# Turning x with 32x32 block transposes on VectorE, and a W stage in eight tiles of 32 rows

## The chip, the cores and the metric

One core of a Trainium2 chip runs the kernel in a single launch. The metric is the device time in microseconds (us), the median of three runs. The engines are TensorE (PE in the profile; its weight loads are listed apart as PEld), VectorE (DVE), ScalarE (ACT), GpSimd (POOL) and SyncE (SP), which here only issues DMA transfers. All data are f32.

## The reference

Two layers over x of 32 images x 128 channels x 64 x 64 pixels. The first layer is the part that matters here: a group norm, then a product with complex 64x64 "butterfly" matrices along both axes of each image, a mix of the channels at each of the 64 x 64 frequencies, the way back, and the sum with x.

```python
def tensor_product(x, tw1, tw2, increasing_stride):
    y = jnp.swapaxes(butterfly_lastdim(jnp.swapaxes(x, -1, -2), tw1, increasing_stride), -1, -2)
    return butterfly_lastdim(y, tw2, increasing_stride)

def _kop2d(x, weight, kd1, kd2, k11, k12, k21, k22):
    ...
    x_f = tensor_product(xc, _c(k11), _c(k12), False)
    w_f = tensor_product(wc, _c(kd1), _c(kd2), False) * math.sqrt(H * W)
    prod = jnp.einsum('bihw,oihw->bohw', x_f, w_f)
    out = tensor_product(prod, _c(k21), _c(k22), True)
    return jnp.real(out)

x = x + _L0_conv_ref(_gn(x), ...)
t = _to_tokens(x)
t = t + _L1_attn_ref(_ln_t(t), ...)
t = t + _L1_ffn_ref(_ln_t(t), ...)      # 8 experts, the best 2 of each token
```

A butterfly is a fixed 64x64 complex matrix, so `x_f` is a real image times one matrix along w and one along h. The change is in the computation of `x_f` alone. The second layer (attention over channels, a mixture of experts) comes after.

## The kernel before

The kernel has three parts, one after the other. The first computes the group norm and `x_f` of each image and stores it to DRAM (`xf`). The second loads `xf` by frequency, makes the frequency's channel matrix and mixes (L632, L654), and stores `pf`. The third goes back from `pf`, adds x and does the second layer (L877 and after). The change is in the first part, lines 131 to 563.

In the first part an image `xs[b]` is [128 channels, 4096 pixels]. Its steps, with the names that the profile shows:

- `load` (L312): eight DMA transfers by SP, into one of three buffers `x`.
- Statistics and norm: eight `bn_stats` on VectorE (L319), the mean over four channels by two small matmuls into a PSUM tile `gps` (L332 and L342), between them and after them short VectorE steps (L337 to L345), a power on POOL (L349), and the scaling in place: four VectorE instructions of 1024 pixels (L362; on ScalarE, L360, for the first four images).
- `turn_over` (L373): the image is turned, so that w lies on the partitions. Four pieces `pz`, each of eight TensorE transposes of 128 x 128, two image rows at a time. `turned` (L383): ScalarE copies each piece out of PSUM in four instructions, into `zs[b]` = [partition: w, once for each half of the channels; channel within its half; h].
- `along_w` (L396): the W stage. Eight pieces `pv`, each of 32 matmuls with 64 rows of contraction, 64 columns and 64 moving columns, placed in four tiles (two of rows by two of columns) of TensorE. The result of a piece is one PSUM tile of two banks. `w_out` (L407): ScalarE copies it into `vs[b]`.
- `along_h` (L418): the H stage. Eight pieces `pf`, each of eight matmuls of 128 x 128 x 128. `h_out` (L428): copied out of PSUM into `f`, six pieces by VectorE, two (`g % 4 == 3`) by ScalarE. `store` (L436): two DMA transfers a piece, by SP.

All PSUM tiles of the part come from one pool of four buffers (`ps`), two banks each, the whole of PSUM. The statistics' `gps` takes one from the first small matmul to the last VectorE step that reads it.

The order of the work is not written out by hand. Each step is added to a `Plan` with an engine, an assumed duration, a due time, the steps it comes after and the buffers that it takes and frees. `Plan.run` then lists the steps: an engine that is free takes the ready step with the earliest due time whose buffers are free. TensorE's steps stay in the order in which they were added (`on_pe`). The assumed durations and the due times (`SLOT` times a place in the loop) only set this order; on the chip an instruction waits for what it needs.

The loop over `s` makes a stage: image s is turned, image s - 1 goes through the W stage, image s - 2 through the H stage, in four quarters: one `pz`, two `pv`, two `pf`. The two small matmuls of image s + 1 stand in the third quarter, on either side of the `pz` and the `pv` (`norm_on_pe`).

The matrix `pw` holds the W stage's butterfly, [64 rows twice, real and imaginary, 64], made by `input_matrices` from a butterfly of a unit matrix (`unit`, `level`); in `unit`, for this butterfly, the even and the odd rows of h are first put in two halves, because a transpose takes two image rows.

Of the kernel before, what the change touches and what calls it, by code (L numbers as in the profile page):

```python
# [90 lines left out]
def kernel(  # L91
# [39 lines left out]
    pw = cp.tile([P, 2, n], F32, name="pw")  # L131
    ph = cp.tile([P, 2, n], F32, name="ph")
# [30 lines left out]
    with ExitStack() as ph1:  # L163
        pp = ph1.enter_context(tc.tile_pool(name="pp1", bufs=4, space=PSUM))
        xp = ph1.enter_context(tc.tile_pool(name="xp1", bufs=3))
        st = ph1.enter_context(tc.tile_pool(name="st1", bufs=1))
        bp = ph1.enter_context(tc.tile_pool(name="bp", bufs=1))
# [3 lines left out]
        SLOT = 27.5  # L171
# [26 lines left out]
        def unit(m, eng):  # L198
            def run():
                cur = tile_of["bf", m] = bp.tile([P, 2, n], F32, tag="bf", bufs=2, name=f"bf{m}_in")  # L200
                eng.tensor_tensor(cur[:, 0, :], ident[:, 0:n], ident[:, n : 2 * n], ALU.add)
                if m == 1:

                    eng.tensor_copy(
                        cur[lo, 0, :].rearrange("p (k r) -> p r k", r=2), ident[lo, 0:n].rearrange("p (r k) -> p r k", r=2)
                    )
                eng.memset(cur[:, 1, :], 0.0)
            return run
# [21 lines left out]
        def input_matrices():  # L230
            xa = tile_of["bf", 1]
            for half in (lo, hi):
                nc.vector.tensor_copy(pw[half], xa[hi])
# [133 lines left out]
        def turn_over(b, g):  # L367
            def run():
                ps = tile_of["pz", b, g] = pp.tile([P, 2, 512], F32, tag="ps", name=f"pz{b}_{g}")
                pv = ps.rearrange("w u (k c) -> w (u k) c", c=P)  # L370
                for k in range(8):
                    h = 2 * (8 * g + k)
                    nc.tensor.transpose(pv[:, k, :], xs[b][:, h * n : (h + 2) * n], ident)  # L373
            return run

        def turned(b, g, r):

            def run():
                if g == 0 and r == 0:
                    zs[b] = zp.tile([P, n, n], F32, tag="z", name=f"z{b}")  # L380
                pv = tile_of["pz", b, g].rearrange("w u (k c) -> w (u k) c", c=P)
                for half in range(2):
                    nc.scalar.copy(  # L383
                        zs[b][half * n : (half + 1) * n, :, 32 * r + 8 * g : 32 * r + 8 * g + 8],
                        pv[r * n : (r + 1) * n, :, half * n : (half + 1) * n].rearrange("w h c -> w c h"),
                    )
            return run

        def along_w(b, g):
            def run():  # L390
                ps = tile_of["pv", b, g] = pp.tile([P, 2, 512], F32, tag="ps", name=f"pv{b}_{g}")
                for k in range(8):
                    for half in range(2):
                        rows = slice(half * n, (half + 1) * n)
                        for r in range(2):
                            nc.tensor.matmul(  # L396
                                ps[r * n : (r + 1) * n, half, k * n : (k + 1) * n],
                                zs[b][rows, 8 * g + k, :], pw[rows, r, :], start=True, stop=True,
                            )
            return run  # L400

        def w_out(b, g):

            def run():
                if g == 0:
                    vs[b] = vp.tile([P, n, P], F32, tag="v", name=f"v{b}")
                nc.scalar.copy(  # L407
                    vs[b].rearrange("h w (a c) -> h w a c", a=2)[:, :, :, 8 * g : 8 * g + 8],
# [15 lines left out]
        def h_out(b, g):  # L424
            def run():
                f = tile_of["f", b, g] = fp.tile([P, 8, 2 * n], F32, tag="f", name=f"f{b}_{g}")
                copy = nc.scalar.copy if g % 4 == 3 else nc.vector.tensor_copy
# [29 lines left out]
        def piece_of_image(b, k):  # L457
# [3 lines left out]
                [("pz", b - 3, g) for g in range(4)] + [("x", b, k - 1), ("pf", b - 4, k)],  # L461
# [28 lines left out]
        def piece(kind, b, g, at):  # L490
            if not 0 <= b < B:
                return
            if kind == "pz":
                add(
                    ("pz", b, g), "PE", 1.0, at, turn_over(b, g), [("nm", b, k) for k in range(4)],
# [948 lines left out]
```

## Time and profile before

| | |
|---|---|
| median of 3 runs | 6062.12 us (6061.84 to 6064.63) |
| span of the profiled execution | 6062.4 us |
| granted TensorE clock, mean | 0.991 |
| TensorE busy over the whole span | 5891.6 us, 97% |
| first part, 60 to 912 us: TensorE / VectorE / ScalarE / POOL busy | 842.2 / 482.5 / 581.2 / 94.1 us of 852 |
| the same: memory traffic | 228 GB/s |
| second part, 912 to 2540 us: TensorE busy | 1623.8 us of 1628 |
| third part, 2540 to 6062 us: TensorE busy | 3399.0 us of 3522 |

The profile is one execution. "Busy" adds the times in which an engine has an instruction in work; matmuls are pipelined, so a busy TensorE is not one at its peak, and the time of one record (220 ns for the W stage) is longer than the distance to the next. In a timeline the columns are start, length, engine, line, operation, output<-inputs, count; square brackets hold the idle time ahead of it and what ended it. "Issue" is idle time in which the engine waited for nothing that the profile shows.

In the first part, sums and means of the groups from 60 to 912 us:

| line, engine | what | count | mean ns of one |
|---|---|---|---|
| L373 PE | transposes `pz` | 952 | 274 |
| L383 ACT | copies of `pz` into `z` | 480 | 580 |
| L396 PE | W stage `pv` | 15,795 | 220 |
| L407 ACT | copies of `pv` into `v` | 248 | 1015 |
| L418 PE | H stage `pf` | 3936 | 278 |
| L428 DVE / ACT | copies of `pf` into `f` | 185 / 61 | 1216 / 1013 |
| L319 DVE | statistics | 224 | 684 |
| L362 DVE | scaling of x | 112 | 840 |

### The profile page before, as it was taken

How to read it: one execution, taken by the hardware profiler on the slowest of the kernel's cores; microseconds unless marked ns; L12 is line 12 of the kernel's file. 1: busy time of each engine (PE TensorE's matmuls, PEld its weight loads, DVE VectorE, ACT ScalarE, POOL GpSimd, SP SyncE). 2: the span in 40 equal slices, each digit the busy share in tenths (PEclk: the TensorE clock that was granted, in tenths of full speed). 3: DMA queues.
4: the chain of work that ended last, by engine and by line, in shares of the span. 5: the costliest groups of instructions: out<-in, count | busy, mean ns of one | idle time of the engine just before them, and what ended most of it. 6: DMA issues, size and time to landing. Idle time of an engine off the chain costs nothing.

```text
span 6062.4 us, 219265 instructions
## 1 busy us (share of the span) xinstructions
PE 5891.6 (97%) x95372; PEld 4677.6 (77%) x95372; DVE 4221.2 (70%) x7696; ACT 3756.5 (62%) x7057; POOL 4191.0 (69%) x3765
## 2 busy tenths in 40 slices
PE   7999999999999999889999999999999999999998
PEld 7999999999999999776666666666666666666654
DVE  5565545555555555448878787787878878787878
ACT  7666664555555555366667667666766766676663
POOL 2110006666666666428898898989989898998988
PEclk9999999999999999999999999999999999999999
DMA  6767666666666666632313222231322223132100
GB/s 200 238 224 237 234 214 193 172 173 172 172 174 171 171 171 172 160 107 77 92 56 102 67 88 81 72 97 57 101 68 84 84 64 104 57 97 71 65 27 28
DMA packets 555044, 756.74 MB, mean 125 GB/s; under 512 B 58592, under 2 KB 319712, under 8 KB 549984
## 3 DMA queue, kind: packets, MB, share of 16 engines
q1 hardware_dynamic: 551856, 738.76, 41.0%
q8 instruction: 749, 12.27, 0.9%
q0 software_dynamic: 896, 2.62, 0.1%
q14 instruction: 215, 1.76, 0.1%
q10 hardware_dynamic: 1328, 1.32, 0.1%
HBM read 406.93 MB, written 335.54 MB: 122 GB/s over the span
## 4 chain that ended last, share of the span: by engine, by line
PE 88%; ACT 7%; issue 2%; DVE 1%; POOL 1%; DMA 1%; SPq 0%; ACTq 0%; POOLq 0%; DVEq 0%
PE pe L1296 28%; PE m L654 17%; PE g L632 9%; PE pf L418 7%; PE pu L877 6%; PE pp L1145 4%; PE py L899 4%; PE pg L1072 4%; PE pv L396 3%; PE px L1283 2%; ACT xn L1273 2%; ACT u L887 2%; PE pz L373 1%; PE pt L1021 1%; ACT z L383 1%
## 5 line engine op out<-in xcount | busy, mean ns | idle before, releaser
L1296 PE MATMUL pe<-ew_sb,xT 128*128 128x512 f32 x4096 | 1948.4, 597 | 18.6 <-DVE tm L1307 15.1
L1307 DVE TENSOR_TENSOR tm<-pe,oh 128x512 f32<-128x512 f32 x2028 | 1346.6, 684 | 478.9 <-PE pe L1296 456.6
L1332 POOL TENSOR_TENSOR tm<-tm 128x512 f32<-128x512 f32 x1014 | 1285.0, 1284 | 202.6 <-DVE tm L1307 199.3
L1296 PEld LDWEIGHTS pe<-ew_sb,xT 128*128 128x128 f32 x4096 | 701.6, 191 | 523.4 <-issue 400.1
L643 DVE COPY f<-g 128x1024 f32<-128x1024 f32 x508 | 622.3, 1225 | 644.4 <-PE g L632 644.2
L654 PE MATMUL m<-f,s 128*64 128x64 f32 x32768 | 1068.9, 224 | 1.1 <-ACT f L643 0.8
L654 PEld LDWEIGHTS m<-f,s 128*64 128x64 f32 x32768 | 999.0, 138 | 62.4 <-issue 1.5
L600 POOL COPY s<-l 128x512 f32<-128x512 f32 x512 | 547.2, 1105 | 526.4 <-issue 509.7
L643 ACT COPY f<-g 128x1024 f32<-128x1024 f32 x508 | 514.7, 1013 | 556.4 <-PE g L632 530.1
L1335 POOL TENSOR_TENSOR tk<-tk,tm 128x256 f32<-128x256 f32 x1014 | 753.9, 743 | 79.5
L1333 POOL TENSOR_TENSOR tm<-tm 128x512 f32<-128x512 f32 x507 | 650.3, 1283 | 39.8
L887 ACT COPY u<-pu 64x512 f32<-64x512 f32 x960 | 556.3, 579 | 135.1 <-PE pu L877 121.6
L632 PE MATMUL g<-c,wst 9*128 9x128 f32 x16256 | 599.6, 283 | 1.7 <-issue 1.5
L632 PEld LDWEIGHTS g<-c,wst 9*128 9x128 f32 x16256 | 503.0, 186 | 36.2 <-issue 1.5
L349 POOL TENSOR_TENSOR grstd<-gms,mhalf 128x1 f32<-128x1 f32 x32 | 17.8, 555 | 737.8 <-DVE gms L345 737.8
L1158 ACT ACTIVATE pp<-pp,m 128x128 f32<-128x128 f32 x1024 | 440.9, 431 | 124.2 <-PE pp L1145 99.2
L602 POOL TENSOR_SCALAR s<-l 128x512 f32<-128x512 f32 x256 | 511.3, 1997 | 0.0
L877 PEld LDWEIGHTS pu<-qw,r 128*128 128x128 f32 x3840 | 455.1, 193 | 62.8 <-ACT u L887 49.0
L877 PE MATMUL pu<-qw,r 128*128 128x128 f32 x3840 | 475.8, 277 | 25.1 <-ACT u L887 25.1
L1289 ACT COPY xT<-px 128x512 f32<-128x512 f32 x256 | 150.2, 587 | 563.2 <-PE px L1283 560.1
L418 PE MATMUL pf<-ph,v 128*128 128x128 f32 x4096 | 491.2, 278 | 6.2 <-issue 1.4
L418 PEld LDWEIGHTS pf<-ph,v 128*128 128x128 f32 x4096 | 467.0, 192 | 16.0 <-ACT z L383 7.1
(169 smaller groups left out, 8569.6 us busy)
## 6 DMA issues: line engine op xcount, KB each, us to landing
xf<-f SPq DMA_DIRECT2D x512, 256.0 KB, 3.3
pf<-o SPq DMA_DIRECT2D x1024, 128.0 KB, 3.3
l<-xf SPq DMA_DIRECT2D x1012, 128.0 KB, 3.2
r<-pf SPq DMA_DIRECT2D x504, 256.0 KB, 4.7
x<-in_x_dram SPq DMA_DIRECT2D x256, 256.0 KB, 4.5
y<-in_x_dram SPq DMA_DIRECT2D x32, 2048.0 KB, 9.3
out_dram<-so SPq DMA_DIRECT2D x256, 256.0 KB, 2.2
tw<-in_tw_dram SPq DMA_DIRECT2D x6, 384.0 KB, 7.5
```

Source lines behind the costliest of these rows:

```text
L418: nc.tensor.matmul(pl[:, j * P : (j + 1) * P], vs[b][:, 8 * g + j, :], ph.rearrange("h r m -> h (r m)"), start=True, stop=True,)
L600: nc.gpsimd.tensor_copy(dst, src)
L632: nc.tensor.matmul(pg[g // 2][:, g % 2, m * P : (m + 1) * P], wst[rows, 16 * half + 4 * t + m, :], c[rows].rearrange("r h k -> r (h k)"), ...
L643: copy(f.rearrange("i m (g o) -> i m g o", g=2), tile_of["g", w, half, t][k].rearrange("i g (o m) -> i m g o", o=4))
L654: nc.tensor.matmul(ps[hh * n : (hh + 1) * n, q, :], s[:, h].rearrange("i k b -> i (k b)")[:, B * r : B * r + n], f[:, h, r, :], start=(r = ...
L877: nc.tensor.matmul(ps[:, k, :], rs[b, e][:, k * P : (k + 1) * P], qw.rearrange("w r m -> w (r m)"), start=True, stop=True,)
L887: nc.scalar.copy(u[r * n : (r + 1) * n, :, oh * n + 8 * e : oh * n + 8 * e + 8], ps[oh * n : (oh + 1) * n, :, r * n : (r + 1) * n].rearran ...
L1296: nc.tensor.matmul(ps, tile_of["xT", b, i // 4][:, i % 4, :], ew_sb[:, es, :].rearrange("d e c -> d (e c)"), start=True, stop=True,)
L1307: nc.vector.tensor_tensor(tile_of["tm", b, i // 2][:, i % 2, es, :], tile_of.pop(("pe", b, i, half)).rearrange("p (e c) -> p e c", c=P), t ...
L1332: nc.gpsimd.tensor_tensor(tm[:, k, 0:4, :], tm[:, k, 0:4, :], tm[:, k, 4:8, :], ALU.add)
L1333: nc.gpsimd.tensor_tensor(tm[:, :, 0:2, :], tm[:, :, 0:2, :], tm[:, :, 2:4, :], ALU.add)
L1335: nc.gpsimd.tensor_tensor(t[:, lo : lo + 2, :], t[:, lo : lo + 2, :], tm[:, :, m, :], ALU.add)
```

## The change

The image is no longer turned by TensorE and ScalarE. Four VectorE instructions an image (`nc.vector.transpose`, pieces `zo`) turn 32 x 32 blocks from SBUF to SBUF: the 32 values of half an image row in 32 channels change places. A block transpose leaves each group of 32 channels on its own 32 partitions, so `zs[b]` becomes [partition: 32 * channel group + w within half a row, channel within its group, half, h].

The W stage's contraction over 64 values of w is therefore two halves of 32, summed in PSUM (`start` for the first, `stop` for the second), with 32 rows of contraction at a time: eight tiles of TensorE, four groups of rows by two of columns, and twice as many matmuls. The four groups of rows write to four PSUM banks, two tiles of the `ps` pool. A piece is four times as many matmuls as before (128) and makes two PSUM tiles, so an image has four pieces.

`pw` grows to hold, on each group of 32 partitions, both halves of the matrix (eight small copies in place of two), and the reordering in `unit` goes. `pw` and `ph` move from the pool of constants to one that ends with the first part.

ScalarE copies four of the eight `pf` pieces instead of two, VectorE four instead of six. In a stage the order on TensorE is now: two W pieces, four H pieces, two W pieces, four H pieces; the two small statistics matmuls stand on either side of the second pair of W pieces. The assumed durations and `SLOT` (27.5 to 23.0) are changed with it. The loads of x wait for the last `zo` of the image three before, where they waited for its `pz`.

```diff
-    pw = cp.tile([P, 2, n], F32, name="pw")
-    ph = cp.tile([P, 2, n], F32, name="ph")
...
+        pw = st.tile([P, 2, 2, n], F32, name="pw")
+        ph = st.tile([P, 2, n], F32, name="ph")
...
-        SLOT = 27.5
+        SLOT = 23.0
...
-                if m == 1:
-
-                    eng.tensor_copy(
-                        cur[lo, 0, :].rearrange("p (k r) -> p r k", r=2), ident[lo, 0:n].rearrange("p (r k) -> p r k", r=2)
-                    )
...
-            for half in (lo, hi):
-                nc.vector.tensor_copy(pw[half], xa[hi])
+            for q in range(4):
+                for half in range(2):
+                    nc.vector.tensor_copy(pw[32 * q : 32 * q + 32, half], xa[n + 32 * half : n + 32 * half + 32])
...
-        def turn_over(b, g):
-            def run():
-                ps = tile_of["pz", b, g] = pp.tile([P, 2, 512], F32, tag="ps", name=f"pz{b}_{g}")
-                pv = ps.rearrange("w u (k c) -> w (u k) c", c=P)
-                for k in range(8):
-                    h = 2 * (8 * g + k)
-                    nc.tensor.transpose(pv[:, k, :], xs[b][:, h * n : (h + 2) * n], ident)
-            return run
-
-        def turned(b, g, r):
...
-                    nc.scalar.copy(
-                        zs[b][half * n : (half + 1) * n, :, 32 * r + 8 * g : 32 * r + 8 * g + 8],
-                        pv[r * n : (r + 1) * n, :, half * n : (half + 1) * n].rearrange("w h c -> w c h"),
-                    )
+        def turned(b, k):
+
+            def run():
+                if k == 0:
+                    zs[b] = zp.tile([P, 32, 2, n], F32, tag="z", name=f"z{b}")
+                nc.vector.transpose(
+                    out=zs[b][:, :, :, 16 * k : 16 * k + 16].rearrange("w c u h -> w h u c"),
+                    in_=xs[b][:, k * 1024 : (k + 1) * 1024].rearrange("c (h u w) -> c h u w", u=2, w=32),
+                )
             return run
 
         def along_w(b, g):
-            def run():
-                ps = tile_of["pv", b, g] = pp.tile([P, 2, 512], F32, tag="ps", name=f"pv{b}_{g}")
+
+            def run():
+                ps = [pp.tile([P, 2, 512], F32, tag="ps", name=f"pv{b}_{g}_{k}") for k in range(2)]
+                tile_of["pv", b, 2 * g], tile_of["pv", b, 2 * g + 1] = ps
                 for k in range(8):
                     for half in range(2):
-                        rows = slice(half * n, (half + 1) * n)
-                        for r in range(2):
-                            nc.tensor.matmul(
-                                ps[r * n : (r + 1) * n, half, k * n : (k + 1) * n],
-                                zs[b][rows, 8 * g + k, :], pw[rows, r, :], start=True, stop=True,
-                            )
+                        for q in range(4):
+                            rows = slice(32 * q, 32 * q + 32)
+                            for r in range(2):
+                                nc.tensor.matmul(
+                                    ps[q // 2][r * n : (r + 1) * n, q % 2, k * n : (k + 1) * n],
+                                    zs[b][rows, 8 * g + k, half, :], pw[rows, half, r, :],
+                                    start=(half == 0), stop=(half == 1),
+                                )
             return run
...
-                copy = nc.scalar.copy if g % 4 == 3 else nc.vector.tensor_copy
+                copy = nc.scalar.copy if g % 2 else nc.vector.tensor_copy
...
-                [("pz", b - 3, g) for g in range(4)] + [("x", b, k - 1), ("pf", b - 4, k)],
+                [("zo", b - 3, 3), ("x", b, k - 1), ("pf", b - 4, k)],
...
+            if kind == "zo":
+                add(
+                    ("zo", b, g), "DVE", 1.2, at, turned(b, g),
+                    [("nm", b, g), ("zo", b, g - 1)] + [("pv", b - 2, k) for k in range(4)], (), ("x",) if g == 3 else (),
+                )
+            elif kind == "pv":
+                add(("pv", b, g), "PE", 2.0, at, along_w(b, g), [("zo", b, k) for k in range(4)] + ["wi"], ("ps", "ps"))
...
-                piece("pz", s, g, at)
-                for k in range(2):
-                    piece("pv", s - 1, 2 * g + k, at + 0.04 + 0.04 * k)
+                piece("zo", s, g, at)
+                if g % 2 == 0:
+                    for k in range(2):
+                        piece("pv", s - 1, g + k, at + 0.04 + 0.08 * k)
```

`w_out` copies each of the two PSUM tiles of a piece as before, one ScalarE instruction a tile, eight an image.

## The prediction

> **What bounds the kernel now.** I read the chain of waits first (88% TensorE), then the stretches: the first part ends near 932 us. The stretch of one image in mid-part, from one start of `pf` piece 0 to the next, shows who is full.
>
> ```profile
> core 0: us, PE busy (x) PEld busy (x) DVE busy (x) ACT busy (x) POOL busy (x), PEclk, DMA share, GB/s
> 551.97:579.39 27.42, 27.32 (x676) 26.29 (x676) 15.94 (x24) 18.90 (x27) 0.55 (x1) 1.00 0.73 242
> ```
>
> TensorE works 27.32 of 27.42 us; VectorE (15.9) and ScalarE (18.9) have room. So in this part an image costs what TensorE's stream costs, and 32 images make up the part after a lead-in. The timeline of that image shows the stream; four such quarters make an image:
>
> ```profile
> 555.53 0.91 PEld L373 LDWEIGHTS pz<-ident,x 128*128 128x128 f32 x8
> 556.61 1.96 PEld L396 LDWEIGHTS pv<-pw,z 64*64 64x64 f32 x128 [0.17 <-issue]
> 558.63 3.65 PEld L418 LDWEIGHTS pf<-ph,v 128*128 128x128 f32 x32
> 562.20 0.91 PEld L373 LDWEIGHTS pz<-ident,x 128*128 128x128 f32 x8
> ```
>
> From start to start: `pz` 1.08, two `pv` pieces 2.02, two `pf` pieces 3.57, together 6.67 us. Four quarters are 26.68; the rest of 27.42, 0.74, are the two statistics matmuls (`gps`). One more reading: an f32 matmul is two weight loads and two matmul records (64 `pv` matmuls: x128 and x128), a transpose one of each.
>
> The third view is where TensorE waits for nothing that has a name. Weight loads at two places of the timeline:
>
> ```profile
> 207.63 1.64 PEld L418 LDWEIGHTS pf<-ph,v 128*128 128x128 f32 x14
> 210.53 1.64 PEld L418 LDWEIGHTS pf<-ph,v 128*128 128x128 f32 x14 [1.26 <-issue]
> ...
> 817.44 1.95 PEld L396 LDWEIGHTS pv<-pw,z 64*64 64x64 f32 x124 [0.17 <-issue]
> 820.30 0.19 PEld L396 LDWEIGHTS pv<-pw,z 64*64 64x64 f32 x4 [0.91 <-issue]
> ```
>
> The stream stops in the middle of a piece, with no semaphore. I counted the weight-load and matmul records before each unnamed stop over 0.3 us between 60 and 912 us. There are eight (0.34 to 1.34 us), and all eight counts leave remainder 193 when divided by 256; none of the thirty-odd stops that a semaphore explains does. The instruction queue's row fits (packets, MB, share of the DMA engines):
>
> ```profile
> q8 instruction: 749, 12.27, 0.9%
> ```
>
> 749 packets of 16,384 bytes over 2 x 95,372 records: 64 bytes a record, 256 records a packet. So TensorE reads its program in blocks of 256 records. The packets' times say how early: a block starts to arrive just after the boundary one block before its own is passed, takes 0.98 us (median; 0.88 to 3.1), and at the eight stops work resumed 1.22 to 1.57 us after the arrival. One block is ahead, then, and no more. From passing a boundary to being able to pass the next took 3.47 to 4.71 us at the eight stops, mean 4.1. Call this time L. Before, it costs next to nothing (18.9 us of unnamed waits of `pv` loads in all, most of them 0.17 us changes of tile), because an image has 1352 records, 5.3 blocks in 27.4 us.
>
> **The change, part by part.** All against the profiled execution: span 6062.4 us, 0.3 us over the runs' median.
>
> *Transposes leave TensorE:* 4 x 1.08 = 4.32 us an image less.
>
> *W stage.* Before, four records start 6.6 ns apart and the next four follow 58.4 ns after: four 64x64 tiles run side by side, a round of 64 columns lasts 58.4. 512 records / 4 x 58.4 = 7.48 us an image. After, 512 matmuls are 1024 records in eight tiles: 8 x 6.6 = 53 ns of starts fit into a round, 1024 / 8 x 58.4 = 7.48 again. The row for four row groups at once is L632 (9 rows, 128 columns): a round each 111.6 ns, as long as one record of L418; row groups do run together.
>
> [...]
>
> *Longer blocks.* A half image is now 512 W records in one run, then four `pf` pieces. A change of tile form costs 0.35 us a round trip (0.095 + 0.048 entering, 0.108 + 0.101 leaving), four times an image before, twice now. Without program reading a half is 3.74 + 0.35 + 7.14 = 11.23, an image 22.46 + 0.74 = 23.2 us.
>
> *Reading the program.* W records, loads counted, go from 1024 to 2048 an image, the transposes' 64 disappear: 2312 in all, nine blocks. A half's W run is 1024 records, so it passes four boundaries. At full rate a block lasts 0.93 us, far under L. The first boundary finds its block present; each of the next three waits L from the one before: 0.93 + 3 L instead of 3.74. No row shows L in a run that always starves. Lower bound: the shortest pieces, start 0.75 (after allowing 48 records that the sequencer is ahead), arrival 0.88, use 1.2: 2.9 us. Upper: the longest stop's 4.7. The eight stops are the long ones by selection, and the traffic gets thinner (some 6.3 MB an image over 41 us, 153 GB/s, against 242), so I take 3.6. Half: 0.93 + 10.8 + 0.35 + 7.14 = 19.2; image 38.4 + 0.74 = 39.2.
>
> [...]
>
> *Clock.* A mostly idle TensorE is slowed:
>
> ```profile
> 2592.28:2595.69 3.41, 0.81 (x28) 0.81 (x29) 0.00 (x0) 0.00 (x0) 0.00 (x0) 1.00 1.02 246
> 2595.69:2599.11 3.42, 3.42 (x72) 3.42 (x70) 1.38 (x2) 0.00 (x0) 0.00 (x0) 0.50 0.75 181
> ```
>
> After 24% work the next 3.41 us have half the clock. A starved W run works 0.93 of 3.6 us, 26%, so some `pf` runs will start slow: from 0 to 3.4 us lost a half (two such windows); I take 1.15, a third, 2.3 an image. Image: 41.5, that is 14.1 more.
>
> *VectorE* gets four 128x1024 block transposes an image and gives two of six L428 copies to ScalarE. No row shows a block transpose.
>
> ```profile
> L600 POOL COPY s<-l 128x512 f32<-128x512 f32 x512 | 547.2, 1105 | 526.4 <-issue 509.7
> L428 DVE COPY f<-pf 128x1024 f32<-128x1024 f32 x192 | 231.1, 1217 | 173.9 <-PE pf L418 164.8 <-ACT v L407 3.9 <-DMA xf<-f 2.3
> L362 DVE TENSOR_SCALAR x<-x,gms,grstd 128x1024 f32<-128x1024 f32 x112 | 87.0, 840 | 19.3 <-POOL grstd L349 19.3
> ```
>
> Bounds: 0.84 (L362, same tile) and 2.2 (twice L600); 1.22 as L428, a plain pass of that size. The rest: 8 x 0.684 statistics, 0.37, 0.7 small, 4 x 0.745 (L362, four in 2.98), 4 x 1.22 = 14.4; with transposes 19.3, at worst 23.2, hidden under 41.5. ScalarE falls to 8 x 1.015 + 4 x 1.013 = 12.2. Neither sets the end.
>
> *New wait.* `gps` holds one of four PSUM slots through both W pieces of the second half (28 images), and these take two each: the second tile of the last piece waits for ScalarE's first L407 copy: 0.22 (the last record's length), 0.13 (until a copy starts, L428 after `pf`), 1.01, 0.05 (until TensorE goes on, L632 after L643) = 1.4 us. Behind it on TensorE stand that piece, `gps` and four `pf`; ScalarE's next copies and VectorE wait for those. While the program starves it is covered (L leaves 2.7 us idle a block); without that cover it costs 1.4.
>
> *Queues and lead-in.* SP issues the same 8 loads and 16 stores an image; the loads' wait moves from `pz` to the transposes, which end in the same stage. q8 gets 120 blocks more, 2 MB. Eight small copies into `pw` instead of two: 6 x 0.23, once. The first image's W stage stood alone (39.4 to 61.8 us) and becomes about 25: lead-in +5 together.
>
> Sum: 31 x 14.1 + 5 = 442; 6062.4 + 442 = 6504 us. Own range: L 2.9 and no slow clock, image 35.0, gives 6302; L 4.7 and 3.4 a half, image 52.6, gives 6847.
>
> **The rivals.**
> First, faster: reading keeps ahead (the eight stops are chance, or a block can be asked for earlier in a run). Then an image is 23.2 + 1.4 = 24.6 in 28 images, 23.2 in three: -28 x 2.8 - 3 x 4.2 + 5 = -86, 5976 us. It decides when L is under 0.93 us. For: 27.4 us of nearly full TensorE lose 4.3. Against: the remainders. A slow transpose (2.2 us, load 23.2 plus waits, say 26.7 an image) would leave 6045.
> Second, slower otherwise: eight tiles run only four at a time, reading hidden: +7.5 an image, 32.1 with the wait; 31 x 4.7 + 5 = 151, 6213. Against: L632.
>
> **How the numbers follow.** Starved reading 0.80, the first rival with its slow form 0.13, the second 0.07. Prediction 6504. The first rival lies outside; below 6200 nothing else does, and I cut the top at 6720, about where L 4.4 with 2 us of slow clock a half stands (image 48.0, 6703). A difference under 0.2% (12 us) can't be told from none: faster 0.12, within 0.01, slower 0.87.
>
> **What would show it.** The W runs should stop with "issue" as the only cause, three times a half, 2.7 us each, 256 records apart; q8 near 870 packets; TensorE's busy share of the part near 60%; PEclk under 1.0 in slices that were 9; VectorE waiting for `pf`. If W runs last 3.8 us with rounds of 58 ns, I am wrong and the time is near 5976; if rounds last 117 ns with no stops, the second rival.

## The result, and the profile after

| | before | after |
|---|---|---|
| median | 6062.44 us | 6707.59 us (6704.58 to 6712.38) |
| ratio, 95% interval | | 1.1066 (1.105 to 1.1081) |
| span of the profiled execution | 6062.4 us | 6702.5 us |
| first `pf` matmul | 61.8 us | 90.1 us |
| mean image: first to last `pf` record, divided by 31 | 28.04 us | 47.68 us |
| first matmul of the second part to the end | 5129.9 us | 5132.7 us |

The changed kernel is 645 us slower; the forecast was 442. In the two traces the difference of 640.1 us is 31 x 19.64 = 609 for the images, 28.3 ahead of the first `pf`, and 2.8 behind the part. So it is all in the first part, and the other two parts were left as they were. (The first to the last `pf` record holds the end of the last stage too; from the first `pf` of the first image to that of the last, the mean image is 0.45 to 0.46 us less in every run below, so the differences are the same.)

The stretch of one image in mid-part, from one first W piece to the next, in the profile of the changed kernel (columns as in the fence of before):

```profile
core 0: us, PE busy (x) PEld busy (x) DVE busy (x) ACT busy (x) POOL busy (x), PEclk, DMA share, GB/s
506.63:552.28 45.65, 33.06 (x1158) 31.53 (x1157) 21.66 (x26) 11.75 (x12) 5.07 (x14) 0.78 0.42 142
```

Where TensorE filled 27.32 of 27.42 us it now fills 33.06 of 45.65, with the clock at 0.78 in place of 1.00. VectorE (21.7) and ScalarE (11.8) have half the time free, memory moves 142 GB/s in place of 242. No engine and no queue is full, yet an image takes 46 us. The weight loads of that image in the timeline of the changed kernel say what it waits for:

```profile
506.63 1.88 PEld L384 LDWEIGHTS pv<-pw,z 32*64 32x64 f32 x170
511.22 1.66 PEld L384 LDWEIGHTS pv<-pw,z 32*64 32x64 f32 x128 [2.70 <-issue]
515.78 2.08 PEld L384 LDWEIGHTS pv<-pw,z 32*64 32x64 f32 x128 [2.91 <-issue]
519.25 1.51 PEld L384 LDWEIGHTS pv<-pw,z 32*64 32x64 f32 x86 [1.39 <-issue]
520.88 8.03 PEld L408 LDWEIGHTS pf<-ph,v 128*128 128x128 f32 x64
528.83 0.30 PEld L328 LDWEIGHTS gps<-gmv,gmean 128*128 128x128 f32 x2
529.15 2.54 PEld L384 LDWEIGHTS pv<-pw,z 32*64 32x64 f32 x232
534.98 0.35 PEld L384 LDWEIGHTS pv<-pw,z 32*64 32x64 f32 x32 [3.29 <-issue]
536.52 1.59 PEld L384 LDWEIGHTS pv<-pw,z 32*64 32x64 f32 x96 [1.19 <-ACT v L397]
538.45 2.08 PEld L384 LDWEIGHTS pv<-pw,z 32*64 32x64 f32 x128 [0.34 <-issue]
542.47 0.52 PEld L384 LDWEIGHTS pv<-pw,z 32*64 32x64 f32 x24 [1.94 <-issue]
```

Read the counts first: 128 weight loads stand between most of the stops, which with their 128 matmuls are 256 records, one block of the program. A W run stops three times, for 1.4 to 3.3 us, with "issue" as the cause. The one stop with another name (`v` L397, 1.19 us) is the new PSUM wait. From 60 to 1560 us I counted all unnamed stops over 1 us: 174, and all 174 at a record count (weight loads, matmuls and TensorE's semaphore instructions) that leaves 193 when divided by 256. From passing such a boundary to passing the next took 4.23 us in the mean: 1.74 until the block starts to arrive, 1.11 to arrive, 1.38 until work resumes. The 10% and 90% points are 3.47 and 5.20.

The waits of the changed kernel from 200 to 1400 us, sorted by their sum (engine, line, what it waited for, total, times, longest):

```profile
ACT v L397 <- PE pv L384: 585.1, 103, 9.6
PEld pv L384 <- issue: 327.3, 143, 4.7
DVE f L418 <- PE pf L408: 325.9, 66, 13.7
...
PEld pv L384 <- ACT v L397: 22.8, 21, 1.2
```

ScalarE waits for W pieces and VectorE for H pieces; TensorE waits 327 us for its own program and 23 us for ScalarE. The slices and the instruction queue on the page of the changed kernel:

```profile
PE   5777767779999999999799999999999999999998
...
PEclk8777777778999999999899999999999999999999
...
q8 instruction: 868, 14.22, 0.9%
```

The first nine slices (168 us each) are 5 to 7, where all but the first were 9, with a clock of 7 to 8; 868 packets stand for 2 x 110,732 records and 804 semaphore instructions, 256 a packet again, and are 119 more than before.

### The profile page after: what moved, and what is told of

Same layout as the page of the kernel before. It is cut to its first block, busy times and chain, and to the rows that moved or that the text cites. A ratio compares the mean times of both kernels' runs of the same rounds, so it can differ in the third digit from the quotient of the medians.

```text
span 6702.5 us, 249448 instructions
## 1 busy us (share of the span) xinstructions
PE 6111.2 (91%) x110732; PEld 4885.6 (73%) x110732; DVE 4381.7 (65%) x7765; ACT 3525.8 (53%) x6609; POOL 4188.4 (62%) x3765
## 4 chain that ended last, share of the span: by engine, by line
PE 84%; issue 8%; ACT 5%; DVE 2%; POOL 1%; DMA 1%; SPq 0%; ACTq 0%; POOLq 0%; DVEq 0%
PE pe L1279 25%; PE m L637 15%; PE g L615 8%; PE pf L408 8%; PE pv L384 7%; PE pu L860 5%; PE pp L1128 4%; PE py L882 4%; PE pg L1055 3%; PE px L1266 1%; ACT xn L1256 1%; ACT u L870 1%; PE pt L1004 1%; PE po L1325 1%; ACT tk L1009 1%
## 5 line engine op out<-in xcount | busy, mean ns | idle before, releaser
L1279 PE MATMUL pe<-ew_sb,xT 128*128 128x512 f32 x4096 | 1946.0, 597 | 19.6 <-DVE tm L1290 16.1
L384 PE MATMUL pv<-pw,z 32*64 32x64 f32 x32768 | 518.1, 281 | 408.1 <-issue 383.4
L384 PEld LDWEIGHTS pv<-pw,z 32*64 32x64 f32 x32768 | 470.1, 171 | 449.1 <-issue 413.9
L397 ACT COPY v<-pv 128x1024 f32<-128x1024 f32 x256 | 248.0, 1015 | 727.7 <-PE pv L384 727.7
L408 PE MATMUL pf<-ph,v 128*128 128x128 f32 x4096 | 579.1, 313 | 2.3 <-ACT v L397 2.2
L408 PEld LDWEIGHTS pf<-ph,v 128*128 128x128 f32 x4096 | 568.9, 228 | 6.2 <-issue 1.4
```

The source lines that it names most:

```text
L384: nc.tensor.matmul(ps[q // 2][r * n : (r + 1) * n, q % 2, k * n : (k + 1) * n], zs[b][rows, 8 * g + k, half, :], pw[rows, half, r, :], sta ...
L408: nc.tensor.matmul(pl[:, j * P : (j + 1) * P], vs[b][:, 8 * g + j, :], ph.rearrange("h r m -> h (r m)"), start=True, stop=True,)
L1279: nc.tensor.matmul(ps, tile_of["xT", b, i // 4][:, i % 4, :], ew_sb[:, es, :].rearrange("d e c -> d (e c)"), start=True, stop=True,)
```

## The experiments

Theory A, the prediction's: TensorE reads its program in blocks of 256 records, one ahead; where 256 records are worked off in less than about 4.2 us it stands still, and the standing still halves its clock. Rival B: matmuls in eight tiles of 32 rows are slow in themselves. Rival C: the long blocks and the PSUM slots they take. Rival D: the block transposes on VectorE. The runs, with the image as above, the program's blocks in an image, and the share of mid-part in which the clock was halved:

| run | median us | ratio to before (95%) | image us | blocks | half clock |
|---|---|---|---|---|---|
| before | 6062.4 | | 28.04 | 5.3 | 0% |
| after | 6707.6 | 1.105 to 1.108 | 47.68 | 9.0 | 53% |
| e1 W in quarters | 6618.4 | 1.090 to 1.094 | 45.27 | 9.0 | 34% |
| e2 half the matmuls | 6181.7 | 1.019 to 1.022 | 31.01 | 5.0 | 27% |
| e3 128 moving columns | 6619.7 | 1.091 to 1.094 | 45.18 | 9.0 | 23% |
| e4 before, matmuls split | 6763.1 | 1.114 to 1.118 | 49.88 | 9.3 | 29% |
| e9 before, 128 columns | 6223.7 | 1.025 to 1.028 | 33.07 | 5.3 | 0% |
| e5 `gps` elsewhere | 6689.2 | 1.102 to 1.106 | 47.12 | 9.0 | 51% |
| e6 W in eighths | 6397.2 | 1.054 to 1.058 | 38.23 | 9.0 | 7% |
| e8 transposes twice | 6722.4 | 1.108 to 1.111 | 48.04 | 9.0 | 54% |
| e7 half the W records | 6069.9 | 1.0005 to 1.0024 | 28.05 | 5.0 | 5% |
| f1 and GpSimd scales | 6053.7 | 0.998 to 1.000 | 27.44 | 5.0 | 5% |
| f2 the same in eighths | 6178.9 | 1.018 to 1.021 | 31.28 | 5.0 | 1% |
| f3 f1, weights later | 6037.7 | 0.995 to 0.997 | 27.12 | 5.0 | 2% |

**e1: the long blocks undone.**

```diff
-                if g % 2 == 0:
-                    for k in range(2):
-                        piece("pv", s - 1, g + k, at + 0.04 + 0.08 * k)
+                piece("pv", s - 1, g, at + 0.04)
```

> The changed kernel (6707.6 us, an image 47.7 us) with the longer blocks undone: one W piece (512 records), then two pf pieces, four times an image; all instructions the same. Theory A (program reading: a block of 256 records can be passed 4.2 us after the one before, mean of 174 stops of the changed kernel, and the idling halves the clock): still nine blocks an image, but two boundaries a run in place of four, so one or two stops a quarter; image 39.5 us at full clock, 44.5 with slow windows, so 6445 to 6605 us. Rival B (matmuls in eight tiles of 32 rows are themselves slow): the same work in another order, 6690 to 6720. Rival C (the long blocks, by the PSUM slots they take, are the whole loss): near or under 6062.

6618.4 us, 13 above A's range; image 45.27. The long blocks cost 2.4 us an image, an eighth of the loss, so C isn't the whole of it, and B's "no change" is out by 70 us. A W run of 512 records now stops once (mean 2.5 us); of the 134 unnamed stops over 1 us from 60 to 1560 us, 133 are at remainder 193.

**e2: half the matmuls.** The second half of the contraction is left out.

```diff
-                    for half in range(2):
+                    for half in range(1):
...
-                                    start=(half == 0), stop=(half == 1),
+                                    start=True, stop=True,
```

> The changed kernel with only the first half of the W stage's contraction: 256 matmuls an image in place of 512, same eight tiles, same blocks, PSUM slots and copies. It leaves out the sum over the other 32 values of w. Theory A: 1288 records an image, five blocks; a W run of 512 records passes two boundaries and stops once; image 28.7 to 30.6 us, so 6100 to 6160 us, and every unnamed stop over 1 us at remainder 193. Rival B: the W run is half as long as now (14.9 to 7.4 us a half image) because its matmuls are half, image 32.8, near 6230, with no stops at block ends. Rival C: blocks and slots are unchanged, so at most the work left out is won (3.7 us an image): 6590.

6181.7 us, 22 above A's range and 48 below B's time; image 31.01. What tells them apart is in the trace of this run, two W runs:

```profile
612.32 1.07 PEld L384 LDWEIGHTS pv<-pw,z 32*64 32x64 f32 x90 [1.54 <-issue]
...
622.64 2.54 PEld L384 LDWEIGHTS pv<-pw,z 32*64 32x64 f32 x228
627.84 0.54 PEld L384 LDWEIGHTS pv<-pw,z 32*64 32x64 f32 x28 [2.66 <-issue]
```

A W run of half an image now has one unnamed stop over 1 us (0.92 in the mean, 2.4 us each) in place of 2.7, and 58 of these 59 are at remainder 193. The eight tiles, the slots and the copies are those of the changed kernel, and 16.7 us an image are gone, where the work left out is 3.7 by the prediction's rate and 5.4 by the measured one (512 matmul records at 10.6 ns, see below).

**e3: more work in the same records.** If the reading sets the W run, work can be added for nothing.

```diff
-        pw = st.tile([P, 2, 2, n], F32, name="pw")
+        pw = st.tile([P, 2, 3, n], F32, name="pw")
...
+                                m = 2 if k < 7 else 1
                                 nc.tensor.matmul(
-                                    ps[q // 2][r * n : (r + 1) * n, q % 2, k * n : (k + 1) * n],
-                                    zs[b][rows, 8 * g + k, half, :], pw[rows, half, r, :],
+                                    ps[q // 2][r * n : (r + 1) * n, q % 2, k * n : (k + m) * n],
+                                    zs[b][rows, 8 * g + k, half, :],
+                                    pw[rows, half, r : r + m, :].rearrange("w m c -> w (m c)"),
```

> The changed kernel with seven of eight W matmuls given 128 moving columns in place of 64 (the second 64 are written over by the next matmul): as many records, nearly twice the TensorE work in the W stage (14.0 us an image at full rate in place of 7.5). Theory A: the work fits into the time that the reading takes (1.87 us of 4.2 a block) and the clock stays higher: W run 0.93 x 2 + 3 x 4.2 = 14.5 us, pf at full clock 7.1, image 44.8 (43 to 47.7): 6610 us (6550 to 6710), so not slower than the changed kernel, and a granted clock over 0.74 in the first part. Rival B (TensorE's work in the tiles sets the run): 6.5 to 15 us an image more, 6915 to 7190.

6619.7 us: 88 us *faster* than the changed kernel, with nearly twice the columns in its W stage. The third part of `pw` repeats its real half, so that each widened matmul has 128 columns to read. B, as a cost of the tiles' work, is out: more work in the tiles can't make a run shorter that the tiles' work sets. Mid-part of the changed kernel and of this run, the same stretch (us, PE, PEld, DVE, ACT, POOL busy, PEclk, DMA share, GB/s):

```profile
300.00:1100.00 800.00, 573.56 (x19238) 548.02 (x19237) 357.06 (x428) 195.07 (x202) 50.96 (x137) 0.74 0.41 136
```

```profile
300.00:1100.00 800.00, 631.27 (x20412) 595.56 (x20412) 378.76 (x454) 207.83 (x215) 50.33 (x135) 0.88 0.43 146
```

TensorE is busier, the clock goes from 0.74 to 0.88, and more records pass in the same time. From 100 to 1350 us a W run, `gps` included, is 15.1 us long in the mean (15.0 in the changed kernel), and a run of `pf` takes 7.5 in place of 8.9. So the gain is the clock of the H stage.

**e4 and e9: the records alone, in the kernel before.** e4 splits each W matmul of before in two of 32 moving columns:

```diff
-                        for r in range(2):
-                            nc.tensor.matmul(
-                                ps[r * n : (r + 1) * n, half, k * n : (k + 1) * n],
-                                zs[b][rows, 8 * g + k, :], pw[rows, r, :], start=True, stop=True,
-                            )
+                        for j in range(2):
+                            for r in range(2):
+                                nc.tensor.matmul(
+                                    ps[r * n : (r + 1) * n, half, k * n + 32 * j : k * n + 32 * j + 32],
+                                    zs[b][rows, 8 * g + k, :], pw[rows, r, 32 * j : 32 * j + 32], start=True, stop=True,
+                                )
```

> The kernel before with each W matmul split into two of 32 moving columns: 2376 records an image in place of 1352 (9.3 blocks), the same columns, the same four 64-row tiles, transposes, order and PSUM slots. Theory A: image 41 to 46 us in place of 27.4: 6500 to 6660 us, with unnamed stops at remainder 193. Rivals B and C, which need the eight tiles or the long blocks: 6050 to 6130.

6763.1 us, over the top of A's range by 103: slower than the changed kernel, without a block transpose, a 32-row tile or a longer W block. In its timeline a quarter with twice the records:

```profile
716.17 0.91 PEld L373 LDWEIGHTS pz<-ident,x 128*128 128x128 f32 x8
717.24 3.37 PEld L397 LDWEIGHTS pv<-pw,z 64*64 64x64 f32 x222 [0.17 <-issue]
722.85 0.65 PEld L397 LDWEIGHTS pv<-pw,z 64*64 64x64 f32 x34 [2.24 <-issue]
```

All 106 unnamed stops over 1 us from 100 to 1500 us are at remainder 193. But 222 loads take 3.37 us, 15 ns each, though each has half the columns: from one matmul record to the next it is 14.6 ns with 64 columns before and 14.6 with 32 here. The split doubled the W stage's TensorE time too, which the expectation had not counted. e9 is the control: more TensorE time, no more records. A matmul gets 128 columns, in one column half of the tiles going up and in the other going down, so that the useless 64 are written over:

```diff
+                            j = 7 - k if r else k
+                            two = k < 7
+                            first, last = (j - r * two, j + 1) if r else (j, j + 1 + two)
                             nc.tensor.matmul(
-                                ps[r * n : (r + 1) * n, half, k * n : (k + 1) * n],
-                                zs[b][rows, 8 * g + k, :], pw[rows, r, :], start=True, stop=True,
+                                ps[r * n : (r + 1) * n, half, first * n : last * n],
+                                zs[b][rows, 8 * g + j, :],
+                                pw[rows, 0:2].rearrange("w m c -> w (m c)") if two else pw[rows, r],
+                                start=True, stop=True,
                             )
```

> A control for the split run (6763 us): its trace has a W matmul record of 32 columns taking as long as one of 64 (14.6 ns from one to the next), so the split doubled the W stage's TensorE work (7.5 to 15 us an image) beside its records. Here the kernel before gets the work without the records: seven of eight W matmuls with 128 moving columns, the second 64 of no use and written over, still 1352 records. Theory A: only the work, 6.5 us an image: image 34, 6270 us (6250 to 6310), no unnamed stops to speak of; the 490 us up to the split run are then its 1024 more records. Rival (the doubled tile time explains the split run): near 6700.

6223.7 us, 26 under the range: image 33.07, +5.0 where 6.5 were expected (four records of 128 columns take 109 ns, so one comes 27.3 ns after the last, not 29). No unnamed stop over 0.3 us from 100 to 850 us, no half clock. The W stage takes 448 x 27.3 + 64 x 14.6 = 13.2 us an image here and 1024 x 14.6 = 15.0 in e4, so about 1.8 of the 16.8 us between the two images are work. The other 15.0 go with 1024 more records: their stops, and the slower clock.

**e5: the PSUM wait.** The statistics' two matmuls go to the last two `pf` pieces of a stage, from the fourth image on.

```diff
-                if g == min(s, 3) - 1:
+                if s < 3 and g == s - 1:
                     norm_on_pe(s + 1, 0)
...
                 for k in range(2):
+                    if s >= 3 and g == 3:
+                        norm_on_pe(s + 1, k)
                     piece("pf", s - 2, 2 * g + k, at + 0.12 + 0.07 * k)
```

> The changed kernel with the two statistics matmuls of an image moved from either side of the second pair of W pieces to the last two pf pieces (from the fourth image on), so that no W piece finds only three PSUM slots. The trace of the changed kernel has 0.59 us a half image of W waits that ScalarE's copies end, 1.2 us an image. Theory A: the wait lies inside a block's reading time for the most part: 0 to 1.2 us an image, 6670 to 6710 us. Rival C (the slot wait starts the loss): more than 40 us faster.

6689.2 us, 18 faster; image 47.12 in place of 47.68. Of 1.2 us of such waits an image 0.6 came back, so half of the wait was covered, and C's slots aren't the loss.

**e6: the records spread.** A W piece is issued in two parts of 64 matmuls, each with one `pf` piece behind it.

```diff
-                for k in range(8):
+                for k in range(4 * part, 4 * part + 4):
...
                 for k in range(2):
+                    piece("pv", s - 1, 2 * g + k, at + 0.04 + 0.1 * k)
                     piece("pf", s - 2, 2 * g + k, at + 0.08 + 0.1 * k)
```

> The changed kernel with the W work spread as evenly as it goes: 64 W matmuls (256 records), one pf piece, eight times an image; the same instructions and copies. Theory A: one boundary in each eighth of some 3.1 us of work, under 4.2, so every block waits for reading and the image is 9.03 blocks x 4.2 = 38 us (31.5 at the shortest stops' 3.47, 42 at 4.66): 6400 us (6190 to 6525), and no order of this work can go below. A rival (run length is all that matters, the number of records is not): the image falls to its work, 26.6 us, near 6030. Rival B (tiles; changes of tile form cost): 0.35 us for each of six more changes, so over the quarters' 6618.

6397.2 us against 6400 expected, and an image of 38.23 us, where 9.03 blocks x 4.23 are 38.2 (from first `pf` to first `pf` 37.77, 4.18 a block). The rival that counts only the length of a run (6030) is out, and so is B (over 6618). Four eighths in the timeline of this run:

```profile
503.51 1.19 PEld L410 LDWEIGHTS pf<-ph,v 128*128 128x128 f32 x10
506.28 0.74 PEld L410 LDWEIGHTS pf<-ph,v 128*128 128x128 f32 x6 [1.58 <-issue]
507.15 1.41 PEld L386 LDWEIGHTS pv<-pw,z 32*64 32x64 f32 x122
510.02 0.20 PEld L386 LDWEIGHTS pv<-pw,z 32*64 32x64 f32 x6 [1.47 <-issue]
510.29 1.86 PEld L410 LDWEIGHTS pf<-ph,v 128*128 128x128 f32 x16
512.27 1.27 PEld L386 LDWEIGHTS pv<-pw,z 32*64 32x64 f32 x106
514.87 0.32 PEld L386 LDWEIGHTS pv<-pw,z 32*64 32x64 f32 x22 [1.32 <-issue]
```

The stops come at the ends of blocks (193 of 194 unnamed ones over 0.3 us from 60 to 1560 us are at remainder 193), also inside `pf` (506.28), where the changed kernel has next to none. The clock is back at full speed in 93% of the time. From 200 to 850 us 103 of 155 block ends show such a stop. The mean from one block end to the next is 4.19 us, with a stop or without; what holds the 52 without one isn't shown. So of the 19.6 us that the change cost an image, 10.2 (38.23 - 28.04) remain however well the records are spread in these tries, and 9.4 came of their bunching: by theory A, blocks that wait while the next ones can't yet be asked for, and the slower clock that follows.

**e8: VectorE.** Every block transpose is issued twice (`for _ in range(2):` around it).

> The changed kernel with every block transpose issued twice (the second writes the same values again): VectorE gets 4 x 1.94 = 7.8 us an image more. Theory A: VectorE is busy 357 of 800 us in mid-part, so it is hidden: 6695 to 6720 us. Rival D (the transposes, 1.94 us in place of the 1.22 assumed, are on the path): up to 250 us slower, 6950.

6722.4 us, 2 over the range. 9.3 of the 15 us are the later first `pf` (99.4 for 90.1 us), the image grew by 0.36 for 7.8 us of VectorE work. D is out: the transposes lie beside the stops.

**e7: the same products in half the records.** A matmul takes both halves of `pw` as 128 moving columns, and the two column halves of the tiles take two channels:

```diff
-                for k in range(8):
+                for k in range(4):
...
-                            for r in range(2):
+                            for j in range(2):
                                 nc.tensor.matmul(
-                                    ps[q // 2][r * n : (r + 1) * n, q % 2, k * n : (k + 1) * n],
-                                    zs[b][rows, 8 * g + k, half, :], pw[rows, half, r, :],
+                                    ps[q // 2][j * n : (j + 1) * n, q % 2, k * P : (k + 1) * P],
+                                    zs[b][rows, 8 * g + 2 * k + j, half, :],
+                                    pw[rows, half].rearrange("w r c -> w (r c)"),
...
-                copy = nc.scalar.copy if g % 2 else nc.vector.tensor_copy
+                copy = nc.scalar.copy
```

A PSUM tile goes out in four copies, since the real and the imaginary part of a channel must move to their own 64 partitions of `vs`; the order is that of e1.

> The changed kernel's transposes, with half as many W instructions for the same products: a matmul takes the real and the imaginary half of pw at once (128 moving columns), and the two column halves of the tiles hold two channels. 256 W matmuls an image, 1288 records, 5 blocks; quarters as in the kernel before. In exchange a PSUM tile is copied out in four copies of 64 partitions (24 an image by ScalarE, 8 by VectorE, 0.6 us each), and all pf copies go to ScalarE: each engine near 22 us an image. Theory A: 1.25 blocks a quarter of 5.8 us, so reading is nearly hidden: image 24.5 to 26.5 us where nothing else waits, 5930 to 6030 us, faster than both kernels; the tight copies may cost up to 3 us an image more, 6120. Rival B (32-row tiles or block transposes are slow in themselves): over 6400.

6069.9 us: 638 us faster than the changed kernel with its transposes and its eight tiles, 0.14% slower than before. B's "over 6400" is out once more. But an image takes 28.05, not 24.5 to 26.5. The waits of this run from 200 to 850 us:

```profile
PEld pv L384 <- issue: 24.4, 21, 2.0
PEld pv L384 <- ACT v L399: 22.6, 27, 2.2
```

The reading still stops it (26 of 27 unnamed stops over 0.4 us from 60 to 1560 us at remainder 193), and W pieces wait for the copies of the last one: ScalarE is busy 79% of mid-part and VectorE 80%, so such copies come late.

**f1, f2, f3: what is left.** Starting from e7, f1 gives the scaling of x to GpSimd, which was mostly idle (busy 30 of 550 us), one `pf` copy in eight to VectorE, and the plan the measured durations:

```diff
-                    nc.vector.tensor_scalar(part, part, v["ms"][:, 0:1], v["rstd"], ALU.subtract, ALU.mult)
+                    nc.gpsimd.tensor_scalar(part, part, v["ms"][:, 0:1], v["rstd"], ALU.subtract, ALU.mult)
...
-        SLOT = 23.0
+        SLOT = 24.5
```

> The version with 128 moving columns (6069.9 us, image 27 to 28.5), with the scaling of x moved from VectorE to GpSimd (idle in this part for 584 of 650 us), one pf copy in eight on VectorE, and durations in the plan as measured (a transpose 1.95). In that version TensorE was busy 92%, VectorE and ScalarE 80 and 79%; waits of an image: 1.9 us for PSUM copies at one W piece, some 1.8 for program reading. Theory A (no single engine is full, the copies come late behind transposes and scaling): VectorE loses 3 us an image, the wait for copies mostly goes: image 25.5 to 27, 5985 to 6040 us. A rival (GpSimd's eight passes of some 2 us an image hold the image back or slow VectorE): 6070 or more.

6053.7 us, 14 over the expected range: most images take 25 to 28 us (mean 27.44), but one takes 43.0. The waits of f1 from 150 to 260 us name it:

```profile
PEld pd L259 <- POOL bf L222: 13.0, 1, 13.0
```

`weight_rows` waits for a butterfly on GpSimd, which the scaling has made late. f2 is f1 with the parts of e6:

> The same with each W piece in two parts of 128 records, a pf piece behind each. Theory A: no two block boundaries then lie less than some 3.1 us of work apart, so the reading stops fall from about 1.8 to under 1 us an image, against 0.17 us for each of eight more changes of tile form (1.4): within 1 us an image of the version with quarters, 5970 to 6060 us. A rival (the reading is hidden already): slower than it by 1.4 us an image, 45 us.

6178.9 us, 119 above the range. The stops at remainder 193 are gone (1 of 25 unnamed ones), yet the image is 31.28: the first part of most W pieces waits 0.8 to 0.9 us for ScalarE's copies (52 us in 650), and ScalarE itself stands still 189 us in that stretch ahead of `pf` copies, without a cause that the profile names. I didn't follow it. f3 is f1 with the weight matrices at the tenth to the 26th image:

```diff
-            if s == 6:
+            if s == 10:
...
-            if 12 <= s < 16:
-                k = s - 12
+            if 22 <= s < 26:
+                k = s - 22
```

> The version with GpSimd's scaling (6053.7 us), with the conv's weight matrices made from the tenth to the 26th image in place of the sixth to the 16th: in its trace one image of 43.0 us stands among images of 26, where TensorE waits 12.8 us for GpSimd's butterfly before the weight matrix. Theory: that wait goes and nothing else changes: 6053.7 - 13 to 17 = 6037 to 6041 us, faster than the kernel before by 0.3 to 0.4%. A rival (the butterfly is late there too, or the later weights collide with the second part): 6050 or more.

6037.7 us, as expected: ratio 0.9961 (0.9948 to 0.9973), 25 us or 0.4% faster than the kernel before. Three quarters in its timeline:

```profile
704.04 3.65 PEld L412 LDWEIGHTS pf<-ph,v 128*128 128x128 f32 x32
707.82 1.85 PEld L384 LDWEIGHTS pv<-pw,z 32*64 32x64 f32 x128
709.84 3.65 PEld L412 LDWEIGHTS pf<-ph,v 128*128 128x128 f32 x32 [0.17 <-issue]
713.41 0.91 PEld L294 LDWEIGHTS pwr<-ident,wr 128*128 128x128 f32 x8
714.48 1.57 PEld L384 LDWEIGHTS pv<-pw,z 32*64 32x64 f32 x104 [0.17 <-ACT f L422]
717.55 0.42 PEld L384 LDWEIGHTS pv<-pw,z 32*64 32x64 f32 x24 [1.50 <-issue]
```

Quarters of 5.8 us where nothing stops (704.04 to 709.84), and one reading stop of 1.5 us. Of the 4.3 us that the transposes took on TensorE before, 0.9 an image are won (28.04 less 27.12). Such stops and waits for copies stand against the rest, how much each wasn't measured, and the first `pf` comes 10 us later than before.

## Why the prediction was right, and where its sizes were off

**The mechanism held.** "One block is ahead, then, and no more": 174 of 174 stops at the remainder that eight stops of before had shown, three a W run, 868 packets where near 870 were forecast. e4 with its control e9, e6 and e7 show it from three sides: more records cost time without any other part of the change, spreading them leaves some 4.2 us a block, halving them gives the loss back. One reading was incomplete: the prediction counts weight loads and matmuls, but the remainder is constant only when TensorE's semaphore instructions are counted too (1053 before, 804 after), and only then are 749 and 868 packets 256 records each.

**L was mis-sized.** The prediction measured 4.1 at eight stops and took 3.6, because long stops were the ones that showed and traffic would be thinner. 174 stops gave 4.23, at 136 GB/s. The eight had been a fair sample, and thinner traffic didn't shorten L. The 48 records allowed in the lower bound of 2.9 were an estimate: in the trace of before the earliest packets start some 41 records ahead of their boundary, 35 in the first part. Three stops a half by 0.63 are 3.8 us an image, 117 us over the part: the largest piece of the 198 missing.

These 4.2 us are a mean at stops of the first part, and no floor of the chip. The second part, which the change leaves alone, passes its records a little faster than that all the time:

```profile
core 0: us, PE busy (x) PEld busy (x) DVE busy (x) ACT busy (x) POOL busy (x), PEclk, DMA share, GB/s
1610.00:3150.00 1540.00, 1539.42 (x47352) 1446.17 (x47349) 906.98 (x741) 782.39 (x862) 1032.96 (x865) 1.00 0.66 170
```

That is the changed kernel: 370 blocks, 4.16 us each in the mean, four in five between 4.05 and 4.28, and only two unnamed stops over 0.15 us. A block there starts to arrive 0.8 us (median) after the boundary one block before its own, not 1.74, and takes 1.14; with the 1.38 until work resumes, L is about 3.3 us there, an estimate. More traffic (170 GB/s) didn't make it longer. Before, the same part ran at the same 4.16 us, so the prediction could have read there that L can be under 4.2.

**The clock was mis-sized.** The prediction let one window in three of a half's `pf` run slow, 1.15 us. The `pf` run took 8.98 us against 7.14, so 1.84 a half, 1.4 an image more than forecast. The clock is halved in 53% of mid-part; from 100 to 1500 us 71% of that time lies inside the W runs (525 of 738 us), where it costs little: e3's W runs are as long at a higher clock.

**The W stage at full rate** was not 7.48 us an image. At full clock the median over 32 records is 10.6 ns from one matmul record to the next, 85 ns a round where 58.4 was forecast: eight tiles do about 1.4 times the records of four in a given time, not twice. A block then takes 1.36 us, under 4.2, so only the first block of a run, which finds its program present, can have cost more: 0.43 us a half at most. In e7, with 128 columns a record, the next record comes after 14.4 ns (27.3 in the four tiles of e9), so there eight tiles do reach nearly twice the rate. The second rival thus had some of the rate right, and the wrong bound.

**The new wait**, 1.4 us and "covered": 0.59 us a half, and e5 shows that half of it was not covered, 0.6 us an image. **VectorE's transpose**, taken at 1.22, takes 1.94 (the same group view of the changed kernel, 100 to 1500 us), near the upper bound of 2.2:

```profile
L368 DVE STREAM_TRANSPOSE z<-x 128x1024 f32<-128x1024 f32 x116 | 223.9, 1942 | 10.8 <-PE pv L384 10.8
```

The cover named for it held (e8). **The lead-in** was put at 5 us and is 28.3. The prediction saw one W stage standing alone ahead of the first `pf`. With two W pieces at a time it is one and a half: 47.3 to 90.1 us, 42.8 where before had 22.4, and it starts 7.9 us later, behind the first transposes.

By halves: W run with `gps` 12.45 forecast (0.93 + 10.8 + 0.35 + 0.37), 14.86 measured; `pf` with its slow clock 8.29 forecast, 8.98 measured. Of the 2.41 us more in a W run 1.89 are L, 0.28 the new wait by e5, and 0.24 are not assigned (the first block can hold them). Twice 3.1 is the 6.2 us between 41.5 and 47.7. The first rival, reading ahead, decides only when L is under 0.93 us; the shortest interval at any of the stops was 2.6. Every size that missed was too low, so the time stands only 12 us inside the top of the range, 6720; that it is inside owes something to where the top was cut.

What stays open: why a block takes 3.5 us in one case and 5 in the next (most of the spread is in the 1.74 us before it starts to arrive), why it starts sooner in the second part, and what holds ScalarE in f2.

## What to carry to other kernels

Count instructions as a resource: in this kernel's first part 256 TensorE records, an f32 matmul being four, took 4.2 us in the mean where the program was late (3.5 to 5.2 in four of five cases), and 4.16 in the second part, where it was in time. So work in small matmuls can be bound by its count, and a change that halves a matmul's contraction doubles that count (the W stage's 1024 records an image became 2048 here). Spread such work between long instructions (e6, 310 us less than the changed kernel), or give each instruction more columns (e7, 638 us less), before moving it to another engine. A stop without a named cause that recurs at one remainder of the record count is the sign to look for, even where it costs nothing yet.

## What the runs showed of the hardware that was not expected

- The half clock comes sooner than at a "mostly idle" TensorE. In windows of 3.41 us of the changed kernel (300 to 1400 us; a matmul counted from its start to the next, at most 115 ns), all 99 windows with under 50% of work were followed by one at half clock, about half of those between 50 and 70%, and 6 of the 102 with over 70%.
- With four tiles of 64 rows, a matmul record of 32 moving columns (e4) takes as long as one of 64 (before): 14.6 ns from one to the next. One of 128 takes 27.3 (e9).
- Added work made a kernel faster (e3, 88 us), by keeping the clock up: 0.88 for 0.74 from 300 to 1100 us, and 1.4 us less for each run of `pf`.
- The program reading isn't one fixed rate: in the second part of the changed kernel a block can be had in some 3.3 us (the estimate above), and 4.16 us a block pass with two stops over 0.15 us in 370 blocks, while at 174 stops of the first part it took 4.23 in the mean, with less memory traffic (136 GB/s from 300 to 1100 us, against 170).
